# Layer 0 of a two-layer image kernel: a row scale applied by GpSimd, plain transposes, a later broadcast of block maxima and earlier gates

## The chip, the cores and the metric

The kernel runs on one NeuronCore of a Trainium2 chip. The metric is the device time of one execution in microseconds (us); the profile shows another execution of the same program, taken by the hardware profiler, and its times are from its span's start.

## The reference

Eight images of 128 x 128 pixels with 128 channels go through two layers, in float32. Layer 0, which the change touches, is linear attention with a layer norm and a residual; layer 1 is a convolution with a four-way selective scan, a gate and a projection.

```python
qkv = einsum('bhwc,cf->bhwf', x, w_qkv); q, k, v = split(qkv, 3)   # 4 heads of 32
q = softmax(q, axis=-2) * 32 ** -0.5        # over the 32 of a head
k = softmax(k, axis=-1)                     # over all 16384 positions
context = einsum('bhdn,bhen->bhde', k, v)
attn = einsum('bhde,bhdn->bhen', context, q)
out = attn @ w_out + b_out
out = (out - mu) * rsqrt(var + 1e-3) * gamma + beta
x = out + x
...
xb, z = split(x @ Win, 2)                   # layer 1
...
out = layernorm(y * silu(z)) @ Wout
```

The split into heads is a reshape without a transpose, so that the kernel's rows stand for what the reference calls channels and the other way round. The gate silu(z) of layer 1 is computed in layer 0, from the image as it is after the residual.

## The kernel before, in words

Layer 0 holds two images in SBUF, each as 128 channels by 16384 positions (`xs`, 8 MB). The work unit is a group of four columns, 512 positions; an image has 32 groups. `image(b)` (L334) walks over slots, 39 of them: in slot t it issues, each for its own group, the stages of the attention of image b (`attend`, L261) and of the context of image b + 1 (`context`, L174), so that the second image's keys and values fill the first one's waits. All is recorded under `in_order` (L62), which ties every engine to the order in which the program issues its instructions. That order is therefore the list of `at(...)` calls in L350 to L374.

Attention of a group, by slot: `query` (L266: TensorE makes pq, VectorE takes the maximum of each head and subtracts it), `exponent` (ScalarE), `normalize` (L277: sums and reciprocal on VectorE, product on GpSimd); a slot later `through_wo` (L284: four matmuls into pg, ScalarE copies it to gt), `through_context` (L292: TensorE makes po, VectorE adds the bias into o, ScalarE squares o), `variance` (L300: VectorE sums the squares); in the next slot `scale` (L305: GpSimd makes 1/sigma with a pow, and a diagonal tile d of identity times 1/sigma), `turn` (L317: four float32 matmuls of o with d, which transpose o and scale it at once); in the slot after that `finish` (L323: gamma and beta on ScalarE, the residual on GpSimd, a store of two groups to DRAM).

Context of a group: `key` (L178), `larger` (L185: running maximum of a block of four groups, at the block's end folded to 128 columns), a slot later `fold` (L199: transpose on TensorE, maximum, a new running maximum m, the rescale factor a, and the diagonal tile dg of m) and `spread` (L216: a matmul of ones with dg, which puts the maxima in every row of pmx; the exponential of a on ScalarE), five slots later `value`, `subtract` and `raise_to` (L223 to L234), then `add` (L236: four matmuls into pc; at a block's end the total takes it up).

Gates: `gate_group` (L147) makes both halves of z for one group: a matmul pz, Silu on ScalarE into a buffer z, and a store of 256 KB from SyncE's queue. z shares a ring of seven buffers with k (tag "k"). For images stored turned (the first four of `ORDER`, L29) VectorE first copies a turned view into v, which shares a ring of three with o (tag "o"), and needs the whole image to be finished. All 32 groups of image b - 1 are issued in a block at the end of slot 0 of image b (L373), which also loads image b + 1 into the space that they free: eight pieces of 1 MB, after every fourth group or, for turned images, at the end. In the last image (b = 7), the gates of images 6 and 7 are spread over the slots, two groups a slot. PSUM has a ring of six buffers for all of pk, pv, pq, pg, po, pt and pz.

Silu and the exponential lie in different function tables of ScalarE; a load of the table (ACT_TABLE_LOAD) is issued where they alternate.

Of the kernel before, what the change touches and what calls it, by code (L numbers as in the profile page):

```python
# [8 lines left out]
F32 = mybir.dt.float32  # L9
BF16 = mybir.dt.bfloat16  # L10
AF = mybir.ActivationFunctionType
ALU = mybir.AluOpType
# [4 lines left out]
P = 128  # L17
B = 8
# [5 lines left out]
K = 4  # L24
GW = 4
GN = GW * H
NG = W // GW
BK = 4
ORDER = (2, 3, 6, 7, 4, 5, 0, 1)  # L29
# [48 lines left out]
def layer0(ctx: ExitStack, tc, xT, w_qkv, w_out, b_out, gamma, beta, win, x1, zs):  # L78
# [12 lines left out]
    nc = tc.nc  # L91
    const = ctx.enter_context(tc.tile_pool(name="l0c", bufs=1))
    wp = ctx.enter_context(tc.tile_pool(name="l0w", bufs=2))
# [4 lines left out]
    ident = const.tile([P, P], F32, name="ident")  # L98
# [40 lines left out]
    def group(b, g):  # L139
        return xs[b % 2][:, g * GW : (g + 1) * GW, :]  # L140

    def load(b, pieces=range(8)):
        for i in pieces:
            s = slice(16 * i, 16 * i + 16)
            nc.sync.dma_start(xs[b % 2][:, s, :], xT[ORDER[b], :, s, :])

    def gate_group(b, g):  # L147

        v = group(b, g)
        if ORDER[b] % K >= 2:  # L150
            v = wp.tile([P, GW, P], F32, name="v", tag="o", bufs=3)
            nc.vector.tensor_copy(
                v, xs[b % 2].rearrange("p w h -> p h w")[:, g * GW : (g + 1) * GW, :]
            )
        for c in range(NC2):
            pz = ps.tile([P, GW, P], F32, name="pz", tag="ps")
            nc.tensor.matmul(pz, wz[:, c * P : c * P + P], v, start=True, stop=True)
            z = wp.tile([P, GW, P], F32, name="z", tag="k", bufs=7)
            nc.scalar.activation(z, pz, AF.Silu)
            dst = zs[ORDER[b], c][:, g * GN : g * GN + GN]  # L160
            nc.sync.dma_start(dst, z.rearrange("p w h -> p (w h)"))

    def gate(b):

        turned = ORDER[b] % K >= 2
        more = b + 2 < B
        for g in range(NG):
            gate_group(b, g)
            if more and not turned and g % 4 == 3:
                load(b + 2, [g // 4])  # L170
        if more and turned:
            load(b + 2)

    def context(b):  # L174

# [85 lines left out]
    def attend(b):  # L261

        cn = ctxs[b % 2]
        qs, gs, os, vs, ys = {}, {}, {}, {}, {}

        def query(g):  # L266
            pq = ps.tile([P, GW * NH, HD], F32, name="pq", tag="ps")
            nc.tensor.matmul(pq, wq[:, 0:P], group(b, g), start=True, stop=True)
            qm = sm.tile([P, GW * NH, 1], F32, name="qm")
            nc.vector.tensor_reduce(qm, pq, AX.X, ALU.max)  # L270
            qs[g] = q = wp.tile([P, GW * NH, HD], F32, name="q", bufs=3)
            nc.vector.tensor_tensor(q, pq, qm.to_broadcast([P, GW * NH, HD]), ALU.subtract)

        def exponent(g):
            nc.scalar.activation(qs[g], qs[g], AF.Exp)

        def normalize(g):  # L277
            q = qs[g]
            t = sm.tile([P, GW * NH, 1], F32, name="qs")
            nc.vector.tensor_reduce(t, q, AX.X, ALU.add)  # L280
            nc.vector.reciprocal(t, t)  # L281
            nc.gpsimd.tensor_tensor(q, q, t.to_broadcast([P, GW * NH, HD]), ALU.mult)  # L282

        def through_wo(g):  # L284
            q = qs.pop(g).rearrange("p (w n) d -> p w (n d)", w=GW)
            pg = ps.tile([P, GW, P], F32, name="pg", tag="ps")
            for i in range(GW):
                nc.tensor.matmul(pg[:, i, :], q[:, i, :], wo, start=True, stop=True)
            gs[g] = gt = wp.tile([P, GW, P], F32, name="gt")
            nc.scalar.copy(gt, pg)  # L290

        def through_context(g):  # L292
            po = ps.tile([P, GW, P], F32, name="po", tag="ps")
            nc.tensor.matmul(po, cn, gs.pop(g), start=True, stop=True)
            os[g] = o = wp.tile([P, GW, P], F32, name="o", bufs=3)
            nc.vector.tensor_tensor(o, po, bb, ALU.add)  # L296
            vs[g] = sq = wp.tile([P, GW, P], F32, name="sq")
            nc.scalar.activation(sq, o, AF.Square)  # L298

        def variance(g):  # L300
            var = sm.tile([P, GW], F32, name="var")
            nc.vector.tensor_reduce(var, vs[g], AX.X, ALU.add)
            vs[g] = var

        def scale(g):  # L305

            var = vs[g]
            nc.gpsimd.tensor_scalar(var, var, 1.0 / P, EPS0, ALU.mult, ALU.add)
            rstd = sm.tile([P, GW, 1], F32, name="rstd")
            nc.gpsimd.tensor_tensor(rstd[:, :, 0], var, half, ALU.pow)  # L310
            vs[g] = d = wp.tile([P, GW, P], F32, name="d")
            i3 = ident.rearrange("p (o c) -> p o c", o=1)
            nc.gpsimd.tensor_tensor(
                d, i3.to_broadcast([P, GW, P]), rstd.to_broadcast([P, GW, P]), ALU.mult
            )

        def turn(g):  # L317
            o, d = os.pop(g), vs.pop(g)
            ys[g] = pt = ps.tile([P, GW, P], F32, name="pt", tag="ps")
            for i in range(GW):  # L320
                nc.tensor.matmul(pt[:, i, :], o[:, i, :], d[:, i, :], start=True, stop=True)

        def finish(g):  # L323
            y = wp.tile([P, GW, P], F32, name="x1t")
            nc.scalar.activation(y, ys.pop(g), AF.Identity, bias=gb[:, 1:2], scale=gb[:, 0:1])
            xg = group(b, g)
            nc.gpsimd.tensor_tensor(xg, y, xg, ALU.add)
            if g % 2 == 1:
                t = xs[b % 2][:, (g - 1) * GW : (g + 1) * GW, :].rearrange("p w h -> p (w h)")
                nc.sync.dma_start(x1[ORDER[b]][:, (g - 1) * GN : (g + 1) * GN], t)  # L330

        return query, exponent, normalize, through_wo, through_context, variance, scale, turn, finish

    def image(b):  # L334

        key = larger = fold = spread = value = subtract = raise_to = add = None
        query = exponent = normalize = through_wo = through_context = None
        variance = scale = turn = finish = None
        later = LATER if b >= 0 else 0
        if b + 1 < B:  # L340
            key, larger, fold, spread, value, subtract, raise_to, add = context(b + 1)
        if b >= 0:
            (query, exponent, normalize, through_wo, through_context, variance, scale, turn,
             finish) = attend(b)

        def at(stage, g):
            if stage is not None and 0 <= g < NG:
                stage(g)

        for t in range(later + NG + BK + 2):  # L350
            a = t - later
            at(scale, t - 2)
            at(finish, t - 3)
            at(query, t)
            if b == B - 1 and t < NG:
                gate_group(b - 1, t)
            at(through_wo, t - 1)
            if b == B - 1 and 4 <= t < NG + 4:
                gate_group(b, t - 4)
            at(exponent, t)  # L360
            at(subtract, a - BK - 1)
            at(raise_to, a - BK - 1)
            at(key, a)
            at(normalize, t)
            at(fold, a - 1)
            at(value, a - BK - 1)
            at(larger, a)
            at(through_context, t - 1)
            at(add, a - BK - 2)
            at(turn, t - 2)  # L370
            at(spread, a - 1)
            at(variance, t - 1)
            if t == 0 and 0 < b < B - 1:  # L373
                gate(b - 1)  # L374

    with in_order(tc):
        load(0)
        load(1)
        for b in range(-1, B):
            image(b)  # L380
# [829 lines left out]
```

## Time and profile before

| | |
|---|---|
| median of 3 runs | 9561.3 us (9557.02 to 9562.55) |
| profiled execution, span | 9556.3 us |
| last gate copy of layer 0 starts | 2351.4 us |
| first keys before image 0, to its first query's maximum | 0 to 112.3 us |
| first query's maximum of images 1 to 7 | 336.5, 623.1, 911.0, 1197.1, 1483.4, 1774.5, 2064.5 us |
| GpSimd ops of layer 0 (mean): pow, diagonal, product with q, residual | 1.02, 1.04, 1.06, 1.27 us |
| table load on ScalarE | 1.28 us |

A time per group of instructions is the mean of one instruction. A wait is idle time of an engine just ahead of an instruction, with the engine and line that ended it. "PE" is TensorE, "PEld" its weight loads, "DVE" VectorE, "ACT" ScalarE, "POOL" GpSimd, "SP" SyncE, whose queue issues the DMAs here. "L288" is line 288 of the kernel before.

### The profile page before, as it was taken

How to read it: one execution, taken by the hardware profiler on the slowest of the kernel's cores; microseconds unless marked ns; L12 is line 12 of the kernel's file. 1: busy time of each engine (PE TensorE's matmuls, PEld its weight loads, DVE VectorE, ACT ScalarE, POOL GpSimd, SP SyncE). 2: the span in 40 equal slices, each digit the busy share in tenths (PEclk: the TensorE clock that was granted, in tenths of full speed). 3: DMA queues.
4: the chain of work that ended last, by engine and by line, in shares of the span. 5: the costliest groups of instructions: out<-in, count | busy, mean ns of one | idle time of the engine just before them, and what ended most of it. 6: DMA issues, size and time to landing. Idle time of an engine off the chain costs nothing. (4 is left out here: it accounts for less than half of the span.)

```text
span 9556.3 us, 89734 instructions
## 1 busy us (share of the span) xinstructions
PE 6281.6 (66%) x24190; PEld 3101.4 (32%) x24352; DVE 8129.7 (85%) x8188; ACT 7202.0 (75%) x8288; POOL 7192.2 (75%) x4361
## 2 busy tenths in 40 slices
PE   8999999898977788777823544636345363543636
PEld 5556655554322233222300311404123040220403
DVE  6667765564988889888979999999999999999996
ACT  5556555567877788777878788888888888888884
POOL 3445544455665578776859999999999999999997
PEclk9999999999988899888955665757557585665857
DMA  2332233313476678987765957759487685867858
GB/s 91 135 133 81 95 133 132 133 71 140 172 266 232 229 262 247 266 263 269 243 204 165 257 174 207 240 174 269 154 228 219 186 260 165 244 190 198 245 165 212
DMA packets 1034807, 1851.21 MB, mean 194 GB/s; under 512 B 274852, under 2 KB 500772, under 8 KB 1026112
## 3 DMA queue, kind: packets, MB, share of 16 engines
q1 hardware_dynamic: 999488, 1711.23, 54.2%
q0 software_dynamic: 34816, 134.23, 7.3%
q8 instruction: 199, 3.26, 0.1%
q14 instruction: 304, 2.49, 0.1%
HBM read 1153.03 MB, written 692.12 MB: 193 GB/s over the span
## 5 line engine op out<-in xcount | busy, mean ns | idle before, releaser
L893 POOL TENSOR_TENSOR ubt<-ubt,sp 128x1024 f32<-128x1024 f32 x1024 | 2457.9, 2458 | 161.0 <-ACT sp L886 74.3
L882 PE MATMUL px<-rows,dtw 128*128 128x512 bf16 x1893 | 909.5, 573 | 2271.7 <-DVE y L943 1063.5
L515 POOL TENSOR_TENSOR tap<-tap 128x1024 f32<-128x1024 f32 x512 | 1206.1, 2367 | 640.1 <-ACT tap L513 517.9
L523 DVE SCALAR_TENSOR_TENSOR acc<-xb,cw,acc 128x1024 f32<-128x1024 f32 x1024 | 1320.6, 1290 | 52.7 <-ACT tap L513 0.9
L886 ACT ACTIVATE sp<-px 128x1024 f32<-128x1024 f32 x1024 | 1046.0, 1024 | 420.7 <-PE px L882 265.6
L951 POOL TENSOR_TENSOR y<-y,ubt 128x512 f32<-128x512 f32 x768 | 1160.0, 1557 | 142.9 <-DVE ubt L924 141.9
L505 PE MATMUL acc<-xi,wt 128*128 128x512 f32 x2048 | 952.2, 608 | 383.9 <-ACT ures L530 383.6
L903 DVE TENSOR_TENSOR_SCAN ubt<-px,ubt 128x1024 f32<-128x1024 f32 x512 | 1177.0, 2332 | 25.9 <-POOL ubt L893 19.2
L901 DVE TENSOR_TENSOR_SCAN ubt<-px,ubt 128x1024 f32<-128x1024 f32 x512 | 1178.3, 2332 | 14.1 <-POOL ubt L893 6.3
L882 PEld LDWEIGHTS <-dtw 128*128 128x128 bf16 x2048 | 163.9, 109 | 3066.2 <-issue 865.9
L890 ACT ACTIVATE px<-sp,sa 128x1024 f32<-128x1024 f32 x1024 | 1110.2, 1109 | 6.1
L513 ACT ACTIVATE tap<-xb,cw 128x1024 f32<-128x1024 f32 x768 | 834.0, 1139 | 68.1 <-POOL tap L515 67.8
L282 POOL TENSOR_TENSOR q<-q,qs 128x512 f32<-128x512 f32 x256 | 271.2, 1060 | 691.5 <-DVE qs L281 691.5
L886 ACT ACT_TABLE_LOAD x512 | 656.9, 1283 | 164.5 <-PE px L882 129.2
L505 PEld LDWEIGHTS acc<-xi,wt 128*128 128x128 f32 x2048 | 383.6, 192 | 928.3 <-ACT ures L530 486.1
L890 ACT ACT_TABLE_LOAD x512 | 656.9, 1283 | 9.2
L1016 PEld LDWEIGHTS px<-wg,z 128*128 128x128 f32 x4096 | 553.8, 218 | 118.6 <-issue 113.5
L909 PE MATMUL pc<-rows,csel 128*128 128x512 bf16 x1017 | 512.7, 585 | 88.9 <-DVE rstd L1004 79.9
L1016 PE MATMUL px<-wg,z 128*128 128x128 f32 x4096 | 554.1, 301 | 0.0
L478 PE MATMUL pxb<-xi,wi 128*128 128x512 f32 x1024 | 495.9, 606 | 4.3 <-ACT xb L487 4.3
L943 DVE TENSOR_TENSOR y<-y,px 128x1024 f32<-128x1024 f32 x384 | 468.7, 1221 | 14.7 <-DVE px L931 0.5
L298 ACT ACTIVATE sq<-o 128x512 f32<-128x512 f32 x256 | 161.2, 630 | 418.2 <-DVE o L296 416.9
(155 smaller groups left out, 15187.7 us busy)
## 6 DMA issues: line engine op xcount, KB each, us to landing
ubt<-ubs SPq DMA_DIRECT2D x512, 1024.0 KB
zs<-z SPq DMA_DIRECT2D x512, 256.0 KB
ubs<-ures SPq DMA_DIRECT2D x256, 512.0 KB
ubs<-turned SPq DMA_DIRECT2D x256, 512.0 KB
z<-zs SPq DMA_DIRECT2D x256, 512.0 KB
y<-gs POOLq DMA_DIRECT2D x128, 1024.0 KB, 10.5
rows<-xps SPq DMA_DIRECT2D x1536, 60.0 KB
xi<-x SPq DMA_DIRECT2D x120, 576.0 KB
```

Of the source, the lines that this page charges most:

```text
L505: nc.tensor.matmul(acc[:, s, :], wt[:, j, c, :], x, start=(j == 0), stop=(j == len(ON_PE) - 1))
L513: nc.scalar.activation(t, at(n, c, *d), AF.Copy, scale=cw[:, c, tap(*d) : tap(*d) + 1])
L515: nc.gpsimd.tensor_tensor(sums[n, c], sums[n, c], t, ALU.add)
L523: nc.vector.scalar_tensor_tensor(acc, at(n, c, *d), cw[:, c, tap(*d) : tap(*d) + 1], acc, ALU.mult, ALU.add)
L882: nc.tensor.matmul(p[:, hf * 512 : hf * 512 + 512], sl.dw[:, c * P : c * P + P], src, start=True, stop=True)
L886: nc.scalar.activation(t, da[n, c], AF.Softplus)
L890: nc.scalar.activation(da[n, c], sp[n, c], AF.Exp, scale=sa[:, sl.s, c : c + 1])
L893: nc.gpsimd.tensor_tensor(ubt[n][:, c, :], ubt[n][:, c, :], sp.pop((n, c)), ALU.mult)
L901: nc.vector.tensor_tensor_scan(e[:, ::-1], x[:, ::-1], e[:, ::-1], start, ALU.mult, ALU.add)
L903: nc.vector.tensor_tensor_scan(e, x, e, start, ALU.mult, ALU.add)
L951: nc.gpsimd.tensor_tensor(v[:, c], v[:, c], h[:, c], ALU.add)
L1016: nc.tensor.matmul(po[:, w, :], z[:, c, w * H : w * H + H], wg[:, c, :], start=(c == 0), stop=(c == NC2 - 1))
```

## The change

Four edits, all in layer 0. `scale` multiplies o by 1/sigma in place on GpSimd, and makes no diagonal tile; `turn` uses TensorE's transpose with the identity. `spread` moves from the end of a slot to the next slot, behind the query. z has a ring of four buffers of its own. The gates of images 0 to 5 begin in the image's own last slots, two groups a slot, from slot 35 (turned) or 33 (not turned) to 38; the remaining 24 or 20 groups come in the block at slot 0 of the next image, as before. The loads for images that aren't turned follow their gates, as before, so that three of eight pieces come early.

```diff
@@ gate_group
-            z = wp.tile([P, GW, P], F32, name="z", tag="k", bufs=7)
+            z = wp.tile([P, GW, P], F32, name="z", bufs=4)
@@ gate
-    def gate(b):
+    gated = [0] * B
+
+    def gate(b, groups):
 
         turned = ORDER[b] % K >= 2
         more = b + 2 < B
-        for g in range(NG):
+        for g in range(gated[b], min(gated[b] + groups, NG)):
             gate_group(b, g)
             if more and not turned and g % 4 == 3:
                 load(b + 2, [g // 4])
-        if more and turned:
-            load(b + 2)
+            if more and turned and g == NG - 1:
+                load(b + 2)
+        gated[b] = min(gated[b] + groups, NG)
@@ scale, turn
-            var = vs[g]
+            var = vs.pop(g)
             nc.gpsimd.tensor_scalar(var, var, 1.0 / P, EPS0, ALU.mult, ALU.add)
             rstd = sm.tile([P, GW, 1], F32, name="rstd")
             nc.gpsimd.tensor_tensor(rstd[:, :, 0], var, half, ALU.pow)
-            vs[g] = d = wp.tile([P, GW, P], F32, name="d")
-            i3 = ident.rearrange("p (o c) -> p o c", o=1)
-            nc.gpsimd.tensor_tensor(
-                d, i3.to_broadcast([P, GW, P]), rstd.to_broadcast([P, GW, P]), ALU.mult
-            )
+            o = os[g]
+            nc.gpsimd.tensor_tensor(o, o, rstd.to_broadcast([P, GW, P]), ALU.mult)
 
         def turn(g):
-            o, d = os.pop(g), vs.pop(g)
+            o = os.pop(g)
             ys[g] = pt = ps.tile([P, GW, P], F32, name="pt", tag="ps")
             for i in range(GW):
-                nc.tensor.matmul(pt[:, i, :], o[:, i, :], d[:, i, :], start=True, stop=True)
+                nc.tensor.transpose(pt[:, i, :], o[:, i, :], ident)
@@ image
             at(query, t)
+            at(spread, a - 2)
...
             at(turn, t - 2)
-            at(spread, a - 1)
             at(variance, t - 1)
             if t == 0 and 0 < b < B - 1:
-                gate(b - 1)
+                gate(b - 1, NG)
+            if 0 <= b < B - 2 and t >= NG + (3 if ORDER[b] % K >= 2 else 1):
+                gate(b, 2)
```

## The prediction

> **What bounds the kernel now.** I first read the slices of the whole execution: the change touches only layer 0, which ends at 2352 us of 9556.3 (the last gate copy of L159 starts at 2351.4), the first ten slices.
>
> ```profile
> span 9556.3 us, 89734 instructions
> ...
> PE   8999999898977788777823544636345363543636
> ...
> DVE  6667765564988889888979999999999999999996
> ACT  5556555567877788777878788888888888888884
> POOL 3445544455665578776859999999999999999997
> PEclk9999999999988899888955665757557585665857
> ```
>
> The reader sees TensorE at 9 of 10 in layer 0, VectorE at 6, and may conclude that TensorE is the bound. The waits of image 0's middle (131 to 310 us) say otherwise. First VectorE's, then TensorE's, in us in total, times, longest:
>
> ```profile
> DVE var L302 <- ACT sq L298: 19.7, 28, 0.8
> DVE qs L280 <- ACT q L275: 2.1, 3, 0.7
> DVE q L272 <- DVE qm L270: 0.5, 1, 0.5
> ```
>
> ```profile
> PE pmx L219 <- DVE dg L214: 7.0, 6, 1.3
> PE pt L321 <- POOL d L313: 2.1, 3, 0.9
> PE pg L288 <- POOL q L282: 0.9, 3, 0.5
> PE po L294 <- ACT gt L290: 0.5, 1, 0.5
> ```
>
> VectorE never waits for TensorE there; TensorE waits for VectorE. The timeline of VectorE through one slot (start, duration):
>
> ```profile
> 235.81 0.68 DVE L296 TENSOR_TENSOR o<-po,bb 128x512 f32<-128x512 f32 x1
> 237.24 0.69 DVE L302 TENSOR_REDUCE var<-sq 128x4 f32<-128x512 f32 x1 [0.76 <-ACT sq L298]
> 237.85 0.68 DVE L270 TENSOR_REDUCE qm<-pq 128x16 f32<-128x512 f32 x1
> ...
> 241.82 1.13 DVE L196 TENSOR_TENSOR run<-run 128x256 f32<-128x256 f32 x1
> ...
> 243.19 0.68 DVE L296 TENSOR_TENSOR o<-po,bb 128x512 f32<-128x512 f32 x1
> ```
>
> This closes a loop: o, its square on ScalarE (the 0.76 wait), var, qm, q, the exponential, sums, reciprocal, maximum, next o. A plain slot's loop is 5.89 us (o at 229.92 to o at 235.81); with the block maxima it is 7.4 and 7.0 us; four slots take 26.16 us. TensorE's own slot is 6.12 us (pg at 231.11 to pg at 237.23), so four slots with the extra transposes and pmx are about 24.9 us, and it is in time everywhere: pq starts at 236.37 and ends at 237.39, its reader qm starts at 237.85; po ends at 234.74, its reader o starts at 235.81. In the two longer slots GpSimd also stands in the loop: after var it does 0.19 + 1.02 + 1.04 + 1.27 + 1.05 us (L308, L310, L313, L327, L282) before L196 or L212 can go on.
>
> TensorE does bound two other places: the end of an image and the gate block. Busy us (count) of PE, PEld, DVE, ACT and POOL in three stretches:
>
> ```profile
> 334.70:340.70 6.00, 0.99 (x5) 0.20 (x3) 4.65 (x12) 1.91 (x2) 0.88 (x1) 0.80 0.00 0
> 326.40:334.70 8.30, 8.30 (x53) 6.35 (x53) 2.83 (x5) 5.21 (x9) 1.49 (x2) 1.00 0.16 63
> 340.70:398.70 58.00, 58.00 (x130) 25.59 (x131) 23.81 (x31) 38.25 (x64) 0.76 (x1) 0.96 0.76 281
> ```
>
> The last slots of an image (second row) and the block of gates (third) leave no TensorE time free; the 5 us between them (first row) are the latency of the next image's first query. The last image is a ScalarE loop of 8.69 us a slot (two table loads of 1.28 each, L159 and L275), in which no TensorE step ends a wait.
>
> **What the Trainium skill says.** TensorE: Matmul & The Clock Gate, Part 4 (PE-mode transpose), has a transpose as one matmul with identity in a mode of its own, and the clock gate not counting it as work. The trace agrees on the first: L206 is a single record of 273 ns where L321 has two. No run here shows the second; TensorE would still have about 5 us of ordinary matmuls in a 5.89 slot. SBUF — State Buffer, "two separate sides", says that GpSimd and a VectorE operation with two SBUF inputs exclude each other for the whole instruction. The trace agrees: L212 (128x1) takes 160 ns before the first image and 970 ns beside GpSimd. ScalarE: Activation LUTs, "What ACT_TABLE_LOAD costs", gives 1283 ns and a drain of about 1380. The trace has 1283 and shows no drain: in image 7 the exponential starts as the load ends (2191.65 + 1.28, 2192.94).
>
> **The change part by part.** Sums are made against the execution's span, 9556.3; the median of the runs, 9561.3, lies 5.0 above it, and I carry this over.
>
> *Real transposes.* L321's eight records at 0.11 us apart (0.89 us) become four single ones. After L206 the next matmul starts 0.11 to 0.14 us later, so four take about 0.5: 0.4 us less of TensorE for each of 256 groups, 100 us in all. In the middle slots it is in time already: nothing comes earlier on VectorE. It counts at an image's end, where pmx and the last values queue behind the last turn (325.44): 7 images x 0.4 = 3 us less.
>
> *1/sigma on GpSimd.* var and pow stay; ident x rstd (1.04 us) becomes o x rstd in place. The nearest row is q x qs, also in place with a broadcast: 1.055. Above, L327 with two full tiles takes 1.27; below, I see no reason for a gain. GpSimd is in the loop in two slots of four, 7 images x 8 blocks x 2 = 112: 112 x 0.015 = 2 us more (0 to 26). The multiplication's new wait is for sq, which var already had. VectorE's o, ring of three, waits as before for a group three slots old.
>
> *Spread a slot later.* TensorE's wait goes: 7.0 us over six blocks, 1.17 each, 56 blocks, 65 us. In the block of the timeline pq ended at 251.67 even with the wait, and qm started at 252.22, behind var. So it is worth nothing; VectorE is late next. Added: pmx between pq and pg. Its reader, L231, comes 1.4 us after qm, pmx is then over by more than a microsecond. The small exponential (0.19, L221) now stands ahead of gt on ScalarE, which waits 0.3 to 0.5 for pg anyway.
>
> *Gates in the last slots.* Two groups a slot: four pz of 0.857, four Silu of 0.60, four stores. TensorE has no hole there, so a gate moved from the block is only moved.
> Images 0 to 3 (turned): 8 groups in four slots, 16 x 0.857 = 13.7 us added, and as much taken from the block. Around it: the first v copy is ready 0.4 us after TensorE; in the last slot the v copy queues on VectorE behind total, reciprocal and four context writes (1.6 us after the last pc), so TensorE waits 2.6; against it, the next query's maximum no longer stands behind those writes (0.8). Sum +2.2 an image, +9. ScalarE has six more table loads, 7.7 us: a slot has 0.63 + 0.59 + 4 x 0.60 + 2 x 1.28 = 6.2 us on ScalarE against 5.2 on TensorE, so it falls behind by 1 us a slot for three slots. Six PSUM buffers let TensorE run ahead five results (4.3 us), which hides it; without that it costs 3.
> Images 4 and 5: 12 groups in six slots, 20.6 us added, and here five slots with reloads use up the lead: I find 1.7 us of wait in the last slot before pc, and gain the 0.8. The block of these images is slower, bound by stores and loads together (ScalarE waits 24.6 us for stores in 1482 to 1556): 32 groups in 68.1 us, 2.13 each, so 12 groups less are 25.5. Net -4 each, -8. SP's queue gets three of eight x loads ahead of the block; they follow stores and reads that are long over.
>
> *Four z buffers for seven.* A store lands 2.03 us after its issue in the turned block (from the semaphore updates in the trace), so a buffer comes back after 0.60 + 0.03 + 2.03 = 2.7 us; four at 0.857 need 3.4. No stall. In the other block it is 6 to 7 us behind a load, but there the transfers bound, not the count; for four cycles I allow 0 to 1 us each, inside the range. In image 7 a slot of 8.69 covers it.
>
> Sum: -3 + 2 + 0 + 9 - 8 = 0; span 9556, time 9561.
>
> **The rivals.** *Faster: TensorE is the bound after all.* For it speaks 168.9 of 179 us busy; against it, that VectorE never waits for it. Then 224 groups x 0.4 and 65 us of waits come off, 155 us: 9406. A part of it if some slots follow TensorE.
> *Slower: the Silu and exponential tables alternate on the path.* Extra loads are 4 x 6 + 2 x 10 = 44, 56.5 us. It decides from the point at which ScalarE's lag passes TensorE's lead of 4.3 us; if pc also waits for k's exponential in each slot, most of it shows. Two thirds shown: 9561 + 38 = 9599; all: 9617.
> *The change doesn't do what it says.* The built order has the four single transposes, pmx behind pq and the gates in the tail, so this falls away.
>
> **How the numbers follow.** No effect in sum 0.62 (own range 9540 to 9582: 3 us each way in six images, and GpSimd's bound); faster 0.16; slower 0.22. A measurement of this kernel can tell about 0.2%, 19 us. Faster by more: the rival and 0.03 of the first, 0.19; slower by more: 0.22 and 0.02, 0.24; between, 0.57. The range goes to 9510 and 9605, which takes the first case whole, most of the slower one and a quarter of the faster; some 0.2 is left out.
>
> **What would show it.** Right: four middle slots still 26.2 us, var's wait for sq still 0.76, TensorE's waits larger, pmx's wait gone, the block shorter by 13.7 and the tail longer by 16. Wrong: middle slots of 5.5 us (TensorE was the bound); L315 near 1.27; ScalarE full in the tail with TensorE waiting for it; z waiting for its stores in the turned blocks.

## The result and the profile after

After: 9568.1 us median (9555.8 to 9576.7), before beside it on the same chip: 9558.3 us (9552.4 to 9568.6). The ratio is 1.0008, 95% interval 1.0002 to 1.0015: slower by about 10 us. That is less than the 0.2% that the prediction held to be measurable, but the interval excludes no change, and the forecast sum was zero. So there is a term to find.

The page of the kernel after, from which line numbers are taken from here on:

```profile
span 9568.6 us, 87983 instructions
...
PE 6266.8 (65%) x23328; PEld 2961.7 (31%) x23328; DVE 8124.3 (85%) x8188; ACT 7247.5 (76%) x8332; POOL 7194.4 (75%) x4361
...
PE   8889888887977787777923543636445363553736
...
DVE  6667765563988899888979999999999999999996
```

TensorE has 862 matmul records less than the 24190 before (the turn's second passes are 256 x 4 = 1024; a trace misses some records), and VectorE's row is as before but for one tenth in one slice. To place the 12.3 us by which the two spans differ, I followed one landmark, the maximum qm of each query, through both traces. "Middle" is an image's fifth to its 32nd query (27 slots), "seam" the last query of an image to the third of the next.

| us | before | after | difference |
|---|---|---|---|
| seven middles, images 0 to 6 | 1232.3 | 1231.9 | -0.4 |
| seams behind images 0 to 3 (turned) | 398.1 | 408.4 | +10.3 |
| seams behind images 4 and 5 | 204.9 | 208.0 | +3.1 |
| seam behind image 6 | 38.4 | 40.0 | +1.6 |
| last gate copy of layer 0 ends | 2352.0 | 2367.2 | +15.2 |
| from there to the end (layer 1) | 7204.3 | 7201.4 | -2.9 |

Layer 1 has the same code in all kernels here; in the 14 traces of this document it takes 7194 to 7211 us, so that 3 us there mean nothing. What the change did to layer 0 lies in the seams: 15.0 of the 15.2 us.

The middle is as it was. VectorE's waits of the kernel after, 131 to 310 us (total, times, longest):

```profile
DVE var L305 <- ACT sq L301: 19.7, 28, 0.8
DVE qs L283 <- ACT q L278: 2.1, 3, 0.7
```

And TensorE's two largest:

```profile
PE pg L291 <- POOL q L285: 6.6, 10, 1.0
PE pmx L222 <- DVE dg L217: 5.6, 6, 0.9
```

VectorE's wait for the square is still 19.7 us in 28 slots, and it still never waits for TensorE. What the transposes freed on TensorE has turned into TensorE's own waiting (pg, 0.9 us before, 6.6 now). The wait of pmx has not gone, as the prediction listed, but only shrunk from 7.0 to 5.6: behind the query it stands early enough to find dg unfinished. The timeline of VectorE shows the loop closed as before:

```profile
235.68 0.68 DVE L299 TENSOR_TENSOR o<-po,bb 128x512 f32<-128x512 f32 x1
237.12 0.69 DVE L305 TENSOR_REDUCE var<-sq 128x4 f32<-128x512 f32 x1 [0.76 <-ACT sq L301]
...
243.07 0.68 DVE L299 TENSOR_TENSOR o<-po,bb 128x512 f32<-128x512 f32 x1
```

o to o is 7.39 us here, 7.38 in the same slot before, with the same 0.76 us of wait.

The seam of image 0, in two parts (last maximum to the next image's first, and from there to its second): busy us (count) of PE, PEld, DVE, ACT and POOL, granted clock, DMA share, GB/s. In the kernel before:

```profile
310.40:336.50 26.10, 22.73 (x129) 16.11 (x127) 14.86 (x31) 14.03 (x26) 12.76 (x14) 1.00 0.11 42
336.50:399.00 62.50, 58.30 (x133) 25.86 (x134) 27.06 (x37) 40.16 (x66) 1.64 (x1) 0.95 0.71 262
```

In the kernel after:

```profile
310.30:353.10 42.80, 36.50 (x145) 21.39 (x143) 20.50 (x40) 29.52 (x48) 12.77 (x14) 0.96 0.30 113
353.10:400.90 47.80, 44.03 (x100) 19.54 (x101) 20.84 (x29) 30.95 (x50) 1.33 (x1) 0.96 0.70 259
```

The block became 14.7 us shorter (forecast 13.7), the tail 16.7 us longer (forecast 16). TensorE is busy 81.0 and 80.5 us in the two sums, as moved work should be; the added 2 us are waiting, as far as one execution tells. TensorE's longest waits in the tail of the kernel after, over the same 42.8 us:

```profile
PE pz L157 <- DVE v L152: 2.5, 1, 2.5
PE pt L321 <- POOL o L315: 2.4, 1, 2.4
```

The first is new, and is the one that the prediction gave 2.6 us. The second stood there before (2.5, for d). Between the two waits the granted clock halves once; the last section comes back to it.

### The profile page after: what moved, and what is told of

The parts are those of the page before. It is cut to its first block, busy times and chain, and to the rows that moved or that the text cites. A ratio compares the mean times of both kernels' runs of the same rounds, so it can differ in the third digit from the quotient of the medians.

```text
span 9568.6 us, 87983 instructions
## 1 busy us (share of the span) xinstructions
PE 6266.8 (65%) x23328; PEld 2961.7 (31%) x23328; DVE 8124.3 (85%) x8188; ACT 7247.5 (76%) x8332; POOL 7194.4 (75%) x4361
## 5 line engine op out<-in xcount | busy, mean ns | idle before, releaser
L884 PE MATMUL px<-rows,dtw 128*128 128x512 bf16 x2048 | 954.1, 565 | 2238.0 <-DVE y L945 1056.0
L905 DVE TENSOR_TENSOR_SCAN ubt<-px,ubt 128x1024 f32<-128x1024 f32 x512 | 1177.0, 2332 | 26.1 <-POOL ubt L895 19.3
L945 DVE TENSOR_TENSOR y<-y,px 128x1024 f32<-128x1024 f32 x384 | 468.7, 1221 | 14.7 <-DVE px L937 0.5
## 6 DMA issues: line engine op xcount, KB each, us to landing
y<-gs POOLq DMA_DIRECT2D x128, 1024.0 KB, 10.6
```

The source lines that it names most:

```text
L884: nc.tensor.matmul(p[:, hf * 512 : hf * 512 + 512], sl.dw[:, c * P : c * P + P], src, start=True, stop=True)
L905: nc.vector.tensor_tensor_scan(e, x, e, start, ALU.mult, ALU.add)
L945: nc.vector.tensor_tensor(v, v, ts.pop(n), ALU.add)
```

## The experiments

The table has every run. Seams and middle are from the profiled execution of each (us, the seams summed, the middle a mean of images 0 to 6); the ratio is to the kernel before, on the same chip. Runs 1, 4 and 7 are single executions. The seams behind images 4 and 5, where loads and stores meet, differ by up to 6 us between executions of the same code (202.7 and 196.3 in runs 8 and 12, whose code differs in the last image alone). The turned ones differ by up to 4 (408.4 and 412.6 in after and run 2, where only the ring differs, which runs 1 and 3 show to be idle there): a stretch of halved clock costs some 1.7 us, and the four turned tails hold three of them in after, six in run 2.

| run | seams 0-3 | seams 4, 5 | middle | last gate ends | median, ratio (95%) |
|---|---|---|---|---|---|
| before | 398.1 | 204.9 | 176.0 | 2352.0 | |
| after | 408.4 | 208.0 | 176.0 | 2367.2 | 9568.1, 1.0008 (1.0002-1.0015) |
| 1 no early gates | 398.2 | 226.3 | 176.0 | 2373.7 | 9582.8, one execution |
| 2 seven z buffers | 412.6 | 194.6 | 175.9 | 2358.4 | 9554.9, 1.0000 (0.9991-1.0009) |
| 3 both of these | 400.1 | 207.1 | 175.9 | 2355.4 | 9556.6, 1.0000 (0.9991-1.0009) |
| 4 no table reload | 411.0 | 205.0 | 176.0 | 2361.8 | 9574.2, one execution |
| 5 sum later | 408.2 | 207.9 | 175.5 | 2370.3 | 9582.2, 1.0024 (1.0016-1.0033) |
| 6 sum later, old turn | 401.7 | 209.4 | 186.7 | 2453.3 | 9657.2, 1.0102 (1.0087-1.0117) |
| 7 gates ahead of add | 398.1 | 196.9 | 176.0 | 2344.2 | 9548.2, one execution |
| 8 turn later | 387.4 | 202.7 | 154.1 | 2265.8 | 9461.6, 0.9903 (0.9890-0.9917) |
| 9 turn later, old turn | 389.9 | 201.5 | 166.7 | 2342.5 | 9534.4, 0.9981 (0.9974-0.9987) |
| 10 turn later and gates | 400.4 | 195.3 | 154.1 | 2267.1 | 9458.3, 0.9900 (0.9886-0.9913) |
| 11 run 7 again | 398.5 | 192.0 | 175.9 | 2340.3 | 9541.7, 0.9986 (0.9979-0.9993) |
| 12 last gates later | 389.2 | 196.3 | 154.1 | 2158.0 | 9363.8, 0.9797 (0.9781-0.9814) |

My theory after reading the two traces: the ring of four z buffers, costed at nothing, took away what the early gates gain behind images 4 and 5. The rivals: the early gates cost it themselves, by their table loads or their place; or the transposes or the later spread cost something.

**Runs 1 to 3: the ring and the early gates, one at a time and together.** Runs 2 and 3 have the first edit of these two, runs 1 and 3 the second.

```diff
-            z = wp.tile([P, GW, P], F32, name="z", bufs=4)
+            z = wp.tile([P, GW, P], F32, name="z", bufs=7)
...
-            if 0 <= b < B - 2 and t >= NG + (3 if ORDER[b] % K >= 2 else 1):
-                gate(b, 2)
```

> The changed kernel without gates in an image's last slots: all 32 groups in the block again, ring of four z buffers. A seam is the time from an image's last query maximum (of 32) to the third query maximum of the next image. Seams before: 99.1 to 100.2 us behind images 0 to 3, 102.9 and 102.0 behind images 4 and 5; after: 100.7 to 103.0, then 103.9 and 104.1. Theory (the early gates cost about 2 us a seam in the turned images, and the ring of four costs about 1.2 us for each 1 MB load in the block of images 4 and 5): seams 0 to 3 near 100, seams 4 and 5 near 110 (seven loads at 10.2 us instead of 9.07), last gate copy near 2373. Rival (the ring of four costs nothing, all of the loss is early gates and their table loads): seams 4 and 5 near 102.5, last gate copy near 2355.

> The changed kernel with seven z buffers in place of four. Theory (ring): loads in the block of images 4 and 5 follow each other in 9.1 us again instead of 10.2, their seams fall from 104 to about 98; seams behind images 0 to 3 stay at 101 to 103; the last gate copy comes near 2355 instead of 2366. Rival (early gates alone cost): no seam moves by more than 1 us, 2366.

> The changed kernel with seven z buffers and no early gates: what is left of the change is the scale on GpSimd with plain transposes, and the later spread. Theory (VectorE's loop bounds the middle of an image, so these two are worth nothing there): 27 slots from the fifth query maximum to the last in 176.0 us as in both kernels, seams as in the kernel before to within 1.5 us, last gate copy 2351 to 2358, ratio 1.000 to 1.001. Rival (TensorE bound): middle slots shorter by some 10 us an image once the early gates are gone.

The ring is what failed. Alone (run 1, against run 3) it costs 19 us at the seams behind images 4 and 5 and nothing at the turned ones; with the early gates (after, against run 2) it costs 13. The medians by themselves could not tell this (the intervals of after and run 2 overlap); the seams can. With seven buffers the early gates gain there 10 us against the kernel before and 12.5 against run 3; the prediction had 8. ScalarE's wait for a store around the block at the start of image 5 (1480 to 1580 us; total, times, longest), first in the kernel before:

```profile
ACT z L159 <- DMA zs<-z: 24.6, 10, 5.3
```

In the kernel after:

```profile
ACT z L159 <- DMA zs<-z: 24.2, 16, 6.1
```

In run 2:

```profile
ACT z L159 <- DMA zs<-z: 18.3, 9, 4.3
```

In run 1 and, below it, in run 3:

```profile
ACT z L159 <- DMA zs<-z: 38.2, 17, 6.1
ACT z L159 <- DMA zs<-z: 28.6, 11, 5.0
```

In the kernel after 12 of the block's 32 groups have gone ahead into the tail, and the wait has not shrunk. Where only the ring differs the totals compare directly: 5.9 us more with four buffers in after than in run 2, of the 7.4 by which the seam behind image 4 differs; 9.6 us more in run 1 than in run 3, of 13.2. The times tell how. In run 2's block Silu makes 7, 8, 8, 8 and 8 results between waits of over 0.3 us: eight are what frees the space for one load of 1 MB. With four buffers in after the first half of the block breaks up into 5, 7, 1, 5, 1 and 2 before it runs in eights as well. As each load is issued behind the gates that free its space, the next load is late too: the eight loads of this image are 9.05 us apart on average before, 10.3 in after and 9.3 in run 2, 10.6 in run 1 and 9.1 in run 3.

Run 3 leaves the transposes, 1/sigma and the later spread of the change alone: ratio 1.0000, middle 175.9. Together they are worth nothing that can be measured here, as forecast.

**Run 4: the early gates without table loads**, by the exponential in place of Silu, handed down to `gate_group`. It leaves out the Silu that the reference asks for in those groups, and is run for its time alone.

```diff
-                gate(b, 2)
+                gate(b, 2, AF.Exp)
```

> The changed kernel with the exponential in place of Silu in the early gates alone (8 of 32 groups of images 0 to 3, 12 of 32 of images 4 and 5 get another function), so that ScalarE loads no tables in those slots. Theory (TensorE sets the pace of these slots, table loads lie beside it): seams 0 to 3 within 0.7 us of the changed kernel's, seams 4 and 5 shorter by at most 1. Rival (tables on the path): 3 to 8 us less at each seam, up to 56 us in all.

The 44 extra table loads of layer 0 are gone (78 in this trace as before the change, 122 in after). The turned seams are 411.0, no shorter than the 408.4 with the loads; single ones moved by up to 4.4 us, more than the 0.7 expected, which is mostly halved clock again (six stretches in the turned tails). The 3 us less behind images 4 and 5 are within the spread of that place. Nothing like the rival's 3 to 8 us a seam appears: the table loads lie beside TensorE's work, and the slower rival falls.

**Runs 7 and 11: seven buffers, and the early gates issued ahead of the context additions**, so that the v copy no longer stands behind the total, the reciprocal and the context writes on VectorE.

```diff
+            if 0 <= b < B - 2 and t >= NG + (3 if ORDER[b] % K >= 2 else 1):
+                gate(b, 2)
             at(add, a - BK - 2)
             at(turn, t - 2)
...
-            if 0 <= b < B - 2 and t >= NG + (3 if ORDER[b] % K >= 2 else 1):
-                gate(b, 2)
```

> The changed kernel with seven z buffers, and the early gates issued ahead of the slot's sum over keys in place of at its end, so that in the last slot the turned copies stand on VectorE before the total, the reciprocal and the context writes. Theory (TensorE's wait of 2.5 us for v in the last slot, and the half clock that follows it, are the loss of images 0 to 3): no such wait, seams 0 to 3 fall from 102 to 104 (with seven buffers) to about 100. Rival (the loss is the table loads): they stay over 102.

> The kernel after with seven z buffers and the early gates issued ahead of the context additions, timed: its one look had the last gate copy of layer 0 end at 2344 us, 8 earlier than in the kernel before. If this holds, the ratio is 0.9985 to 0.9998, faster than before by a little; if the one look was luck, 0.9995 to 1.001.

The tail of run 7, to be read beside the 2.5 us of after:

```profile
PE pz L157 <- DVE v L152: 0.9, 1, 0.9
```

The turned seams are back at 398.1 (run 2: 412.6), and with 20 executions the kernel is faster than before by 0.14% (0.07 to 0.21). So the position within the slot was the cost of the early gates behind turned images, and the ring their cost behind the other two. Not all of the 14 us against run 2 is the wait itself: the wait takes 1.6 us less a seam, and with it all six stretches of halved clock of run 2's turned tails are gone, an estimate of 10 us at the 1.7 us of the last section.

**Runs 5 and 6: is VectorE's loop really what holds the middle?** If it is, taking the wait for the square out of it must shorten the slot. Run 5 (on run 3's kernel) moves the sum of squares a slot later, behind the next query's maximum, and scale with it; run 6 does this to the kernel before.

```diff
-            at(scale, t - 2)
...
             at(query, t)
+            at(variance, t - 2)
+            at(scale, t - 2)
...
-            at(variance, t - 1)
```

> The kernel of the third run (plain transposes, later spread, seven z buffers, no early gates), and besides the sum of squares of a group a slot later, behind the next query, with 1/sigma after it, so that VectorE doesn't wait 0.76 us a slot for the square. Theory (VectorE's loop o, square, sum, query bounds the middle slots, and TensorE comes next): with four transposes TensorE needs about 5.7 us a slot, the 27 middle slots fall from 176 to about 160 us, seven images give some 110 us, ratio 0.987 to 0.990. Rival (TensorE or GpSimd's chain already bounds the slots, the wait only fills): 172 to 176 us, ratio over 0.996.

> The kernel before with the same move of the sum of squares and nothing else: the turn is still a matmul with the diagonal tile. Theory: TensorE now bounds at about 6.1 us a slot, four slots in 24.9 us, the 27 middle slots in about 168 us, ratio near 0.994, so that the plain transposes are worth about 8 us an image only here, where VectorE no longer waits. Rival (transposes are worth nothing, also then): the same middle slots as with transposes, 160 us.

A miss: the middle is 175.5 us for 160, and the time rises by 0.24%, since most tails take some 3 us longer than in run 3 (28.9 for 25.5), each with a stretch at half clock. The wait for the square is gone, but another has its place. VectorE's largest wait in run 5, 131 to 280 us:

```profile
DVE qm L273 <- PE pq L271: 21.1, 16, 2.3
```

And TensorE's, in the same stretch:

```profile
PE pt L321 <- POOL o L315: 15.5, 20, 2.1
```

Now the turn stands in the same slot as the sum it waits for: pq, qm, q, var, GpSimd's pow and product, turn, and behind the turn, in TensorE's order, the next pq. For the first time the middle shows VectorE waiting for TensorE. In this loop the diagonal turn is slower: run 6 has 186.7, 11.2 us more in 27 slots, 0.41 a slot. That is what the prediction had for the transposes (0.4) where TensorE counts. The two runs also differ in the place of spread, but TensorE shows no wait for pmx in run 6.

**Runs 8 and 9: both loops opened.** Sum and scale a slot later as in run 5, scale behind normalize, and turn and finish a slot later too. Run 8 is on run 3's kernel, run 9 makes the same moves in the kernel before.

```diff
-            at(scale, t - 2)
-            at(finish, t - 3)
+            at(finish, t - 4)
             at(query, t)
+            at(variance, t - 2)
...
             at(normalize, t)
+            at(scale, t - 2)
...
-            at(turn, t - 2)
-            at(variance, t - 1)
+            at(turn, t - 3)
```

> The kernel after with seven z buffers, no early gates, and two moves together: the sum of squares (variance) goes behind the next slot's query, and 1/sigma, scale and turn follow it so that the turn is a whole slot behind the sum; finish is a slot later still. My theory (the middle slot is a loop through VectorE that waits for ScalarE's square; in the run that moved the sum alone, the turn stood behind GpSimd in the same slot and closed another loop through TensorE) expects both waits gone: TensorE at about 5.66 us a slot bounds, the 27 middle slots of an image fall from 176 us to 156 to 164, and the total to about 9470 (ratio 0.987 to 0.993). The rival, that some third loop of the same length is behind these two (GpSimd's chain of q product, pow, scale and residual, or the PSUM ring of six), expects the middle at 172 or more and the ratio at 0.998 or above.

> The kernel before (diagonal tile, two-pass turn, spread at the end of the slot) with the same moves as in the run above. If TensorE bounds once both loops are open, the old turn costs 0.4 us a slot and the old place of spread 1.17 us a block of four slots: the middle is 168 to 176 us, some 11 to 18 above the run with the plain transposes, and the ratio 0.993 to 1.000. If TensorE doesn't bound even then, the middle is within 2 us of the other run's.

The middle falls from 175.9 to 154.1, a little below the expected 156 to 164. Busy us (count) in 135 to 280 us, columns as above, in the kernel after:

```profile
135.00:280.00 145.00, 133.14 (x612) 79.16 (x611) 120.55 (x209) 87.31 (x157) 100.08 (x112) 1.00 0.10 41
```

And in run 8:

```profile
135.00:280.00 145.00, 143.31 (x711) 93.82 (x710) 130.72 (x240) 98.53 (x179) 117.09 (x129) 1.00 0.12 48
```

TensorE is busy 143.3 of 145 us: it has become the bound, and only now the transposes are worth something. Run 9, with the diagonal turn and the old place of spread, has 166.7, just under the expected 168: 12.6 us more than run 8, 0.47 a slot. Of that the transposes are 0.4 by the count of the prediction; little is left for the later spread, whose wait (pmx, 7.0 us in before) is down to 0.8 in run 9 without moving it. Its 65 us in the faster rival were for the most part a wait that goes by itself once VectorE isn't late.

But the total of run 8 gained 93 us only, where seven middles gave 153. That the ratio still lies in the expected range is luck: the middles gave more than expected, and the last image gave back what nobody had counted. Its 27 slots took 317.3 us for 234.7. TensorE's waits there, 2080 to 2200 us:

```profile
PE pz L157 <- POOL x L327: 24.5, 10, 2.4
```

The gate of a group in the last image was four slots behind its query, and finish now stands in that same slot, so each pz waits for the residual on GpSimd.

**Run 10: run 8 with the early gates of run 7.**

> The kernel of the first run of this batch with the early gates as well, issued ahead of the last slots' context additions. The seams are work of TensorE alone, so the gain of the early gates there (8 us in the run that had them ahead of the additions) should add to the gain in the middle: 6 to 10 us below the first run, ratio 0.986 to 0.992, below both kernels. Rival: the tail's slots now lack the place for the gates, since the turn of the last groups ends a slot later, and the two gains do not add (within 2 us of the first run).

A miss: 3 us in the median with overlapping intervals, and the last gate ends no earlier. The turned seams lost 13 us (387.4 to 400.4), those behind images 4 and 5 gained 7, hardly more than their spread. The trace of run 10 shows the rival's reason. The gates of a turned image need the whole image, and finish is now a slot later; at image 0's first early gate VectorE's copy waits for the last residual on GpSimd, and TensorE for the copy:

```profile
303.85 1.38 DVE L152 COPY v<-x 128x512 f32<-128x512 f32 x2 [1.70 <-POOL x L327]
304.64 5.40 PE L157 MATMUL pz<-v,wz 128*128 128x512 f32 x8 [2.17 <-DVE v L152]
```

Four such waits of 2.2 us (one in each turned tail), and a stretch of halved clock in two of the tails, are by estimate some 12 of the 13 us. That starting these gates a slot later would take it away was not tried.

**Run 12: run 8, and the last image's gates a slot later.**

```diff
-            if b == B - 1 and 4 <= t < NG + 4:
-                gate_group(b, t - 4)
+            if b == B - 1 and 5 <= t < NG + 5:
+                gate_group(b, t - 5)
```

> The kernel with the later turn (plain transposes, seven z buffers, no early gates), and in the last image the gate of a group one slot later, five slots behind its query for four. In the later-turn kernel the last image's slots grew from 8.7 to 11.5 us, with TensorE waiting 2.5 us a slot at the gate's matmul for the residual on GpSimd (L327), which that kernel makes in the same slot. My theory: with the extra slot this wait goes, and the last image's 27 slots return from 317 us to about 235, so that layer 0 ends some 80 us earlier and the ratio is 0.981 to 0.984. Rival: the slots of the last image stay above 10 us, because the wait is only a sign of ScalarE's table loads standing elsewhere in the slot; then the ratio stays at 0.988 to 0.991.

The 27 slots are back at 234.2 us, and the pz wait is all but gone (1.2 us from 2080 us to layer 0's end at 2158). The slots behind the last query, where the same wait stood, shrank by 18 us as well (43.2 to 24.8), which I had not counted; hence 0.9797 where 0.981 was the lower end. This kernel is 2.0% faster than the kernel before and beats both.

## Why the prediction was right or wrong

**Wrong: "No stall. In the other block it is 6 to 7 us behind a load, but there the transfers bound, not the count".** The transfers do hold this block, with seven buffers too (18.3 us of waits for stores in run 2); that the count doesn't matter was wrong. Stores of this block land 7.1 us after their issue in the median of the kernel before, and eight results are needed to free the space for the next load; with four buffers Silu stops in between and waits for a store. The waits are chained to the loads, so that the count of buffers helps to set how early the next load is issued, although transfers take up the time. The prediction allowed 0 to 1 us for each of four cycles and put it into the range only. The step that then fails in its sum is "12 groups less are 25.5": up to the image's third maximum the two blocks became 18.7 and 19.3 us shorter, and with seven buffers 26.1 and 23.6. The term is 13 us with the early gates (19 without). "Net -4 each, -8" therefore came out as +3.1, and with seven buffers as -10.3. These 11 us are most of the 15 by which layer 0 ends later. For the turned blocks "No stall" holds: in image 0's, ScalarE waits 0.3 us for a store.

**Right in the wait, in the total partly by luck: the turned seams.** Forecast +2.2 each, +9 in all; measured +10.3, with the wait for v forecast as 2.6 and measured as 2.5. But the prediction has no term for the halved clock, which the four tails show three times after (5 us) and once before (1.4): without it some 6.6 us are left, against 9 less the 1.6 that the -3 gives these four. Run 7 takes the v wait down to 0.9, and cost and halved clock go with it.

**Right: the middle.** Nothing for the transposes, nothing for the later spread, 2 (0 to 26) for GpSimd's product: measured -0.4 in all. o times rstd takes 1.040 us in the middle of image 0, as long as the diagonal did (1.04), so the upper end of 1.27 was idle. Runs 5, 6, 8 and 9 show the reason given, VectorE's loop, and not only the result. The loop can be opened, and then the faster rival's mechanism holds at once; its size, 155 us, took the block maxima's 65 us along, which run 9 shows to be no cost of spread's place.

**Right, but covered: the -3 at the images' ends.** Without early gates a tail is 25.5 us in most images (runs 1 and 3) for 26.1 before, the forecast 0.4 and a little more. In the others it is 27.2 or 27.0, by a halved clock (below), and in sum little is left of it. Of the +1.6 behind image 6, 1.1 is this (a tail of 27.2 for 26.1); no term of the prediction had it.

**Right: the table loads** are hidden (run 4).

**Not counted: the last image** could lose or gain 100 us, more than the change moved at all seams together, by one slot of distance between finish and gate (runs 8 and 12). The change doesn't touch that distance, so it cost the prediction nothing.

## What to carry to other kernels

Where a ring of buffers is emptied behind large loads on the same queue, count the results that are made between two loads (here eight) and not only the time of a lone store; and where the load waits for those results, ask whether too few buffers delay the load too, even where "the transfers bound". Here four buffers were too few and seven enough; five and six were not tried. TensorE, busy 9 of 10, was not the bound of these slots, where VectorE never waited for it: find the loop first, move the step that waits a slot later together with all that hangs on it, and only then pay for making the busy engine cheaper. After each such move look at the one special stage (here the last image) in which the moved step may have met its consumer.

## What of the hardware was not expected

Where TensorE waited some 2.4 us in a tail, its clock was in some tails halved for a stretch right behind. The tail of image 0 in run 1, columns as above:

```profile
310.00:336.00 26.00, 20.80 (x112) 14.03 (x110) 15.33 (x31) 13.95 (x25) 12.77 (x14) 1.00 0.10 41
```

And in run 3, which differs in z's ring alone:

```profile
310.20:336.30 26.10, 22.04 (x111) 14.97 (x109) 13.82 (x28) 13.77 (x25) 12.47 (x13) 0.93 0.10 40
```

The column after POOL's is the granted clock: 1.00, and 0.93 over 26.1 us, which is one stretch of 3.4 us at half (3.4 x 0.5 / 26.1 = 0.07). The tail is 25.5 us in the first and 27.2 in the second, so it costs 1.7. In the kernel after, such a stretch lasts from 326.6 to 330.0 us, and a group of eight pc takes 1.93 us there for 1.06 outside it.

The Trainium skill, TensorE: Matmul & The Clock Gate, Part 1 (The HAM clock gate), has windows of 3413 ns that run freely and half rate after an idle one. The traces agree on the length: between the first change of the clock and the last, every stretch of all 14 traces is a whole multiple of 3.41 us. But no wait of these tails lasts that long. What counts as idle can be read by laying the grid of these windows over layer 0 of all 14 traces and taking TensorE's busy share in each window at full clock. Of the windows with less than 0.41, all 279 were followed by half rate; of those with more than 0.51, none of 8504; between the two both occur (50 of 138 were). A wait of 2.4 us that falls into one window is enough, one that two windows share need not be. Since the grid lies differently in each execution, the same code meets both cases, as runs 1 and 3 do in this tail.

The transposes count like other work in this. In the kernel after, the window ahead of the stretch in image 0's tail holds four transposes, but the one in image 1's tail, around the wait for v, holds none. Both, in order of time, are followed by half rate (from 326.6 and from 637.2 us):

```profile
323.20:326.61 3.41, 1.34 (x8) 1.10 (x9) 1.21 (x6) 1.69 (x3) 3.17 (x3) 1.00 0.00 0
633.80:637.21 3.41, 0.94 (x9) 0.75 (x7) 2.34 (x8) 1.79 (x4) 0.00 (x0) 1.00 0.67 249
```

Run 1's window around the same wait in image 0 is not:

```profile
322.90:326.31 3.41, 1.48 (x8) 1.10 (x9) 1.21 (x5) 1.80 (x4) 3.03 (x3) 1.00 0.00 0
```

It is busy for 0.43 of its length, the other two for 0.39 and 0.28. Without its transposes it would hold some 0.28 of ordinary work, a share at which windows without transposes were always followed by half rate (58 of 58 between 0.27 and 0.35). Part 4 of that page has transposes not count as work for the clock in the same way; for staying at full clock the traces do not bear this out. What a plain turn does change is the share: four transposes are busy for 0.66 us behind this wait, where the eight records of the diagonal turn took 1.16. Before the change one tail of seven held a stretch at half clock, in the kernel after five.

GpSimd's pow keeps VectorE out less than its length says. In run 5 two engines' timelines overlap so:

```profile
248.22 1.02 POOL L313 TENSOR_TENSOR rstd<-var,half 128x4 f32<-128x4 f32 x1
...
248.88 0.16 DVE L213 TENSOR_TENSOR m<-m 128x1 f32<-128x1 f32 x1
249.07 0.16 DVE L215 TENSOR_TENSOR a<-m 128x1 f32<-128x1 f32 x1
```

Both small operations take their full speed, 0.16 us, inside the pow's 1.02, where the prediction had 0.97 beside GpSimd and the Trainium skill, SBUF — State Buffer, "two separate sides", an exclusion for the whole instruction. It is no single case: in run 5's trace all 82 of these 128x1 operations that start inside a pow take 0.16 us, and in the kernel before all 14, where the 42 that start inside the product with q take 0.97. Here the measurement decides: the exclusion does not show for this pow on 128x4.
